# Key differences through all eight steps of an attention unit, and row maxima turned by VectorE and DMAs through DRAM

## The chip, the core and the metric

The kernel runs on one core of a Trainium2 chip. TensorE multiplies matrices, VectorE (DVE), ScalarE (ACT) and GpSimd (POOL) work element by element, and SyncE (SP) issues the DMAs. The metric is the time of the whole program on the device in microseconds, lower is better.

## What is computed

One decoder layer without biases on x of shape (2, 2048, 512) in float32: self-attention with 16 heads of width 32 and rotary angles, a cross-attention of width 77 in the form of two matmuls with a gelu between, and a feed-forward part whose weights are only signs. Each part takes the layer norm of x and is added to x.

```python
x = x + attn(layernorm(x))      # below
x = x + gelu(layernorm(x) @ ctx.T) @ ctx                 # ctx: (2, 77, 512)
x = x + clip((layernorm(x) @ sign(W).T) * scale + bias, -100, 100)

def attn(x):                    # H = 16, DK = 32, S = 2048
    Q = rope(heads(x @ W_q.T)); K = rope(heads(x @ W_k.T)); V = heads(x @ W_v.T)
    scores = Q @ K.T / sqrt(DK)
    return merge(softmax(scores) @ V) @ W_o.T
```

## The kernel before

The work goes batch by batch, and in a batch in two stages: `project_batch` makes Q, K (turned so that the head's 32 values lie on partitions) and V from 16 chunks of 128 tokens; then `Attention.run` goes over 32 *units*. A unit is 256 queries (half of a block of 512) times a group of four heads, which lie on the four quarters of the 128 partitions, so that matmuls of two heads can run beside each other.

A unit has eight *steps* (`STEPS`); step i handles 256 keys: block `i % 4` of 512 keys, chunks 0 and 1 of it in steps 0 to 3, chunks 2 and 3 in steps 4 to 7 (`chunk`). Each step has two halves, heads 0 and 1 first, then heads 2 and 3. A half issues, in this order: the scores of its two heads for the first chunk of keys, the *maxima* matmuls of the other two heads for a later unit, the scores for the second chunk, the exponentials on ScalarE (line 705), the addition of the two chunks' exponentials on GpSimd (`sm`, line 707), the reductions of the maxima on VectorE (line 484), and the matmuls of the step before: `weigh` (weights times values, line 583) and `total` (the softmax's sums, line 597).

The softmax needs the row maxima before the scores. `maxima` therefore computes query times key once more with queries on partitions (line 472), and VectorE reduces each 128x512 tile to one column. This runs `AHEAD` = 10 steps ahead of the scores; the first ten steps of a batch are done by `lead` within and at the end of `project_batch`, whose last stretch is ordered by hand. After the last maximum of a unit `split_maxima` takes the negated maximum of the four blocks (line 491) and splits it on GpSimd into three bfloat16 parts (lines 493 to 497) in `mt`, a tile of 128x2x4x32 whose other entries are zero. `turn_maxima` brings the maxima from columns to rows: one transposing DMA on SP's queue (line 504), and for a batch's first unit two TensorE transposes.

`lower` opens the PSUM tile `st` of a head with a matmul of ones by these rows (line 550), which writes the negated maximum everywhere; `scores` then adds query times key to it. In steps 1 to 3 and 5 to 7 the keys are the differences between a block and the one before (`dk`, made by GpSimd in `key_steps`), so that adding them to what stands in PSUM turns the last step's scores into this step's. Steps 0 and 4 start anew:

```python
if i % NB == 0:
    self.lower(u, heads)
```

PSUM has three tiles for `ps` of the maxima (`ps_s`), four for `st` (`ps_t`), one for `acc`. `divide` takes the reciprocals of the sums on VectorE (line 617). The rest of the layer, `after_attention`, is cut into pieces that `background` slips between the halves: projections (382, 408, 363), norms (327, 137, 138) and the stores. Within `run` the order of TensorE, VectorE, ScalarE and GpSimd is the order of the program text; SP's queue is ordered by the scheduler.

Of the kernel before, what the change touches and what calls it, by code (L numbers as in the profile page):

```python
# [9 lines left out]
F32 = mybir.dt.float32  # L10
F32R = mybir.dt.float32r
BF16 = mybir.dt.bfloat16
AF = mybir.ActivationFunctionType
ALU = mybir.AluOpType
# [11 lines left out]
HQ = 256  # L26
NU = NB * ND * 2
STEPS = NCH // 2
AHEAD = STEPS + 2
SCALE = 1.0 / math.sqrt(DK)  # L30
EPS = 1e-5
MAX_VAL = 100.0
# [4 lines left out]
def decoder_layer(  # L37
# [48 lines left out]

    x_next = [load_x(0, 0), load_x(0, 1)]
    qkv = load_qkv()
    cos = const.tile([P, NCH, DK // 2], F32, tag="cos", name="cos")
    sin = const.tile([P, NCH, DK // 2], F32, tag="sin", name="sin")  # L90
    nc.sync.dma_start(cos, rope_cos.rearrange("(p c) d -> p c d", p=P))
    nc.sync.dma_start(sin, rope_sin.rearrange("(p c) d -> p c d", p=P))

    ident = const.tile([P, P], F32, tag="ident", name="ident")
    make_identity(nc, ident)
# [7 lines left out]
    nc.scalar.activation(minus_half, ones[:, :CPB], AF.Identity, scale=-0.5)  # L103


    mts = []
    for n in range(2):
        mt = const.tile([P, 2, 4, DK], BF16, tag=f"mt{n}", name=f"mt{n}")
        nc.vector.memset(mt, 0.0)
        mts.append(mt)  # L110

    late = {}

# [63 lines left out]

    def project_batch(b, ahead, att, xnt, wk, wq, wv):  # L180
        def times(dst, xnt, w, part=range(ND)):
            for i in part:
                nc.tensor.matmul(dst, xnt[:, i, :], w[:, i, :], start=(i == 0), stop=(i == ND - 1))  # L183

        def transpose_qk(ch, qk, which=(0, 1)):
            blk, c = divmod(ch, CPB)
            cols = slice(c * P, (c + 1) * P)
            for a in which:
                pt = ps_s.tile([P, ND, P], F32, tag="s", name="ptqk")
                for i in range(ND):  # L190
                    nc.tensor.transpose(pt[:, i, :], qk[:, a, i * P : (i + 1) * P], ident)  # L191
                (nc.vector.tensor_copy if a else nc.scalar.copy)((att.q, att.k)[a][blk][:, :, cols], pt)
            if c == CPB - 1 and 1 in which:
                att.open_block(blk)

        def values(ch, xnt, pool=None):
            pv = (pool or ps_s).tile([P, D], F32, tag="t" if pool else "s", name="pv")
            times(pv, xnt, wv)
            keep_values(ch, pv)

        def keep_values(ch, pv):
            v = kvq.tile([P, D], F32, tag=f"v{ch}", name=f"v_{b}_{ch}")
            nc.scalar.copy(v, pv)
            att.v.append(v)


        def rotate(ch, a, ps, r):
            half = [P, H, DK // 2]
            cs = cos[:, ch, None, :, None].to_broadcast(half + [2])
            sn = sin[:, ch, None, :].to_broadcast(half)  # L210
            pairs = ps.rearrange("p (h i t) -> p h i t", i=DK // 2, t=2)
            t1 = r[:, 0, a, :].rearrange("p (h i t) -> p h i t", i=DK // 2, t=2)
            t2 = r[:, 1, a, :].rearrange("p (h i t) -> p h i t", i=DK // 2, t=2)
            nc.vector.tensor_tensor(t1, pairs, cs, ALU.mult)
            nc.vector.scalar_tensor_tensor(
                t2[:, :, :, 0], pairs[:, :, :, 1], -1.0, sn, ALU.mult, ALU.mult
            )
            nc.vector.tensor_tensor(t2[:, :, :, 1], pairs[:, :, :, 0], sn, ALU.mult)  # L218
            nc.gpsimd.tensor_add(r[:, 0, a], r[:, 0, a], r[:, 1, a])  # L219

        held = None
        for ch in range(NCH):
            if ch == (NB - 1) * CPB:
                drain()
            blk, c = divmod(ch, CPB)
            if c == 0:
                att.q.append(kvq.tile([P, ND, BLK], F32, tag=f"q{blk}", name=f"q_{b}_{blk}"))
                att.k.append(kvq.tile([P, ND, BLK], F32, tag=f"k{blk}", name=f"k_{b}_{blk}"))
            r = big.tile([P, 2, 2, D], F32, tag="s", name="r")
            xn = norm(ahead, b, ch + 1) if ch + 1 < NCH else None  # L230
            pk = ps_t.tile([P, D], F32, tag="t", name="pk")
            pq = ps_t.tile([P, D], F32, tag="t", name="pq")
            if ch == NCH - 1:
                break
            times(pk, xnt, wk)
            rotate(ch, 1, pk, r)
            att.lead(1)
            background_between(2)
            times(pq, xnt, wq)
            rotate(ch, 0, pq, r)  # L240
            background_between(2)
            if held is not None:
                transpose_qk(*held)
            held = (ch, r[:, 0])
            xnt_next = turn(xn)
            if ch < NCH - 2:
                values(ch, xnt)
            else:
                left = xnt
            background_between(2)  # L250
            xnt = xnt_next


        ordered = tc.manual_schedule(
            engines={mybir.EngineType.PE, mybir.EngineType.DVE}
        )
        ordered.__enter__()
        times(pk, xnt, wk)
        rotate(ch, 1, pk, r)
        transpose_qk(*held)  # L260
        times(pq, xnt, wq)
        transpose_qk(ch, r[:, 0], (1,))
        rotate(ch, 0, pq, r)
        pv = ps_t.tile([P, D], F32, tag="t", name="pv")
        times(pv, left, wv, (0,))
        att.lead(1)
        times(pv, left, wv, range(1, ND))
        keep_values(ch - 1, pv)
        att.lead(AHEAD)
        values(ch, xnt, ps_t)  # L270
        transpose_qk(ch, r[:, 0], (0,))
        att.split_maxima(0)
        att.turn_maxima(0)
        ordered.__exit__(None, None, None)
        att.key_steps()
# [169 lines left out]
    class Attention:  # L445
# [13 lines left out]
        def maxima(self, n, heads):  # L459
# [25 lines left out]

            return reduce

        def split_maxima(self, u):
            mx = self.mx.pop(u)
            neg = small.tile([P, 2, 4], F32, tag="neg", name="neg")  # L490
            nc.vector.tensor_reduce(neg, mx, AX.X, ALU.max, negate=True)
            mt = mts[u % 2]
            nc.gpsimd.tensor_copy(mt[:, :, :, 0], neg)
            nc.gpsimd.tensor_tensor(neg, neg, mt[:, :, :, 0], ALU.subtract)
            nc.gpsimd.tensor_copy(mt[:, :, :, 1], neg)
            nc.gpsimd.tensor_tensor(neg, neg, mt[:, :, :, 1], ALU.subtract)
            nc.gpsimd.tensor_copy(mt[:, :, :, 2], neg)


        def turn_maxima(self, u):  # L500
            mt = mts[u % 2]
            mrow = small.tile([P, 2, P], BF16, tag="mrow", name="mrow")
            if u > 0:
                nc.sync.dma_start_transpose(mrow, mt.rearrange("p c h d -> p (c h d)"))
            else:
                pt = ps_s.tile([P, 2, P], BF16, tag="s", name="ptm")
                for c in range(2):
                    nc.tensor.transpose(
                        pt[:, c, :], mt[:, c].rearrange("p h d -> p (h d)"), ident_b
                    )  # L510
                nc.vector.tensor_copy(mrow, pt)
            self.mrow[u] = mrow.rearrange("p c q -> p (c q)")

        def key_steps(self):
            self.dk = [None] + [
                const.tile([P, ND, BLK], F32, tag=f"w{n}", name=f"dk{n}") for n in "kqv"
            ]

            def differences(g):
                for kb in range(1, NB):
# [11 lines left out]
            for _ in differences(0):  # L534
                pass
            queue.append(others())


        @staticmethod
# [19 lines left out]
        def scores(self, u, i, heads, c):  # L559
            qb, g, hf = self.units[u]  # L560
            kb, kc = divmod(self.chunk(i, c), CPB)
            keys = self.dk[kb] if kb else self.k[kb]
            for h in heads:
                r = self.rows[h]
                nc.tensor.matmul(  # L565
# [81 lines left out]
        def run(self):  # L647
# [37 lines left out]
            for t in range(NU * STEPS):  # L685
# [10 lines left out]
                pw = big.tile([P, 4, 2, HQ], F32, tag="s", name="pw")  # L696
                sm = sums.tile([P, 4, HQ], F32, tag="sm", name="sm")
                for heads, others in (((0, 1), (2, 3)), ((2, 3), (0, 1))):
                    if i % NB == 0:
                        self.lower(u, heads)  # L700
                    self.scores(u, i, heads, 0)
                    reduce = self.maxima(t + AHEAD, others)
                    self.scores(u, i, heads, 1)
# [6 lines left out]
                    if heads[0] == 0:  # L710
                        first_half()
                        finish()
                        if u >= NU - ND:
                            background(1)
                        elif t % 2 == 1:
                            background(1, light=True)
                    else:
# [3 lines left out]
                            finish()  # L721
                        if (t + AHEAD) % STEPS == STEPS - 1 and u + 1 < NU:
                            self.split_maxima(u + 1)
                            self.turn_maxima(u + 1)
                        background(1)
                prev = (u, i, pw, sm)
            xnt = turn(xn) if more else None
# [9 lines left out]
    xnt = turn(norm(x_next, 0, 0, nc.vector))  # L737
    for b in range(B):
        att = Attention(b)
        project_batch(b, x_next, att, xnt, *qkv)  # L740
        if b == 0:
            late_loads()
        load_ctx(b)
        xnt = att.run()
        if b + 1 < B:
            x_next = att.x_next
            qkv = load_qkv()
    alone.append(True)
    queue += tail
    while queue:  # L750
# [49 lines left out]
```

## Time and profile before

| | before |
|---|---|
| time, median of 3 runs | 2693.01 us (2692.51 to 2693.29) |
| the profiled execution | 2693.15 us, of it 2691.0 us span |
| TensorE clock granted | 0.998 |
| TensorE (PE) busy | 2668.3 us, 99% |
| VectorE (DVE) busy | 1710.0 us, 64% |
| GpSimd (POOL) busy | 1732.8 us, 64% |
| ScalarE (ACT) busy | 1321.0 us, 49% |
| DMA queues of the kernel's data | 4.8% of 16 engines |

The span runs from the first to the last instruction. A matmul's end is modelled, so a busy TensorE is not one at its peak. A line of the timeline gives start and length in microseconds, engine, source line, operation, names of what is written and read, number of instructions merged, and in brackets the idle time before it and what ended it. A line of the groups gives busy time, mean nanoseconds of one instruction, idle time before, and its releasers.

### The profile page before, as it was taken

Reading aid. Unit: us, or ns where it says so; the run is one execution under the profiler, and the core shown is the slowest. Engines: PE = TensorE matmul, PEld = TensorE weight load, DVE = VectorE, ACT = ScalarE, POOL = GpSimd, SP = SyncE. Lnnn points to the kernel's source line nnn. Section 1 sums busy time; section 2 is a strip of 40 time slices with the busy share of each in tenths; the row PEclk is TensorE's granted clock in tenths of the full one; section 3 lists DMA queues with packets and bytes.
Section 4 is the critical chain, followed back from the end, with each engine's and each line's share of the span. In section 5 each row is a group of like instructions: output and inputs, shape, how many; then the busy total and the mean of one; then the engine's idle time right before and its main releaser. Section 6 shows DMA issues by size and latency. Waiting matters only on the chain.

```text
span 2691.0 us, 70222 instructions
## 1 busy us (share of the span) xinstructions
PE 2668.3 (99%) x30756; PEld 1490.3 (55%) x30756; DVE 1710.0 (64%) x2863; ACT 1321.0 (49%) x2394; POOL 1732.8 (64%) x1876
## 2 busy tenths in 40 slices
PE   8999999999999999999999999999999999999998
PEld 4445555555555555555554455555565555555555
DVE  3447777676766766676344477766767667766754
ACT  2115555455546554555422155555555455546553
POOL 3227777567857785677543287766687567857772
PEclk9999999999999999999999999999999999999999
DMA  3010000000000000000201000000000000000000
GB/s 126 24 32 2 5 4 4 4 4 18 20 3 4 12 28 3 4 12 26 73 25 40 5 4 4 4 4 4 4 27 12 4 4 19 19 4 4 19 19 17
DMA packets 38019, 43.54 MB, mean 16 GB/s; under 512 B 20662, under 2 KB 20918, under 8 KB 37712
## 3 DMA queue, kind: packets, MB, share of 16 engines
q1 hardware_dynamic: 37712, 39.05, 4.8%
q8 instruction: 241, 3.95, 0.6%
q14 instruction: 66, 0.54, 0.1%
HBM read 26.58 MB, written 8.39 MB: 13 GB/s over the span
## 4 chain that ended last, share of the span: by engine, by line
PE 98%; DVE 1%; DMA 0%; issue 0%; ACT 0%; POOL 0%; SPq 0%; POOLq 0%; ACTq 0%
PE st L565 23%; PE acc L583 22%; PE ps L472 18%; PE acc L597 8%; PE po L382 4%; PE pk L183 4%; PE pq L183 4%; PE pv L183 4%; PE st L550 3%; PE pf L363 2%; PE pt L345 1%; PE po L408 1%; PE ptqk L191 1%; PE ph L389 1%; PE pt L173 1%; DMA wk<-in_wk_t_dram 0%
## 5 line engine op out<-in xcount | busy, mean ns | idle before, releaser
L707 POOL TENSOR_TENSOR sm<-pw 128x512 f32<-128x512 f32 x1024 | 1295.2, 1272 | 599.5 <-ACT pw L705 596.8
L484 DVE TENSOR_REDUCE mx<-ps 128x1 f32<-128x512 f32 x2048 | 1308.9, 682 | 513.0 <-PE ps L472 509.1
L705 ACT ACTIVATE pw<-st 128x512 f32<-128x512 f32 x2048 | 1111.4, 595 | 947.0 <-PE ps L472 619.4
L472 PE MATMUL ps<-k,q 32*128 32x512 f32 x4096 | 1187.8, 640 | 0.0
L583 PE MATMUL acc<-pw,v 128*32 128x256 f32 x8192 | 655.1, 391 | 0.0
L597 PE MATMUL acc<-sm,ones 128*32 128x128 f32 x7680 | 388.8, 280 | 0.0
L583 PEld LDWEIGHTS acc<-pw,v 128*32 128x32 f32 x8192 | 162.5, 108 | 396.6 <-issue 378.3
L472 PEld LDWEIGHTS ps<-k,q 32*128 32x128 f32 x4096 | 352.4, 183 | 20.2 <-issue 13.8
L597 PEld LDWEIGHTS acc<-sm,ones 128*32 128x32 f32 x7680 | 248.6, 110 | 153.2
L565 PE MATMUL st<-q,dkk 32*128 32x256 f32 x2048 | 291.2, 400 | 0.0
L565 PE MATMUL st<-q,dkq 32*128 32x256 f32 x2048 | 290.0, 400 | 0.0
L565 PE MATMUL st<-q,dkv 32*128 32x256 f32 x2048 | 290.0, 400 | 0.0
L565 PE MATMUL st<-q,k 32*128 32x256 f32 x2048 | 262.8, 375 | 0.0
L565 PEld LDWEIGHTS st<-q,dkk 32*128 32x128 f32 x2048 | 175.8, 184 | 89.5 <-issue 51.3
L565 PEld LDWEIGHTS st<-q,dkq 32*128 32x128 f32 x2048 | 173.0, 184 | 79.9 <-issue 54.1
L565 PEld LDWEIGHTS st<-q,dkv 32*128 32x128 f32 x2048 | 175.0, 184 | 58.6 <-issue 26.3
L565 PEld LDWEIGHTS st<-q,k 32*128 32x128 f32 x2048 | 195.4, 187 | 14.0
L219 POOL TENSOR_TENSOR r<-r 128x512 f32<-128x512 f32 x64 | 81.1, 1268 | 161.8 <-DVE r L218 151.5
L617 DVE RECIPROCAL num<-num 128x128 f32<-128x128 f32 x128 | 120.4, 942 | 53.5 <-ACT num L611 53.5
L137 DVE BATCH_NORM_STATS2 st<-x 128x6 f32<-128x512 f32 x96 | 65.4, 686 | 91.7 <-DMA x<-in_x_dram 91.4
L183 PE MATMUL pk<-wk,xnt 128*128 128x512 f32 x256 | 118.2, 606 | 2.4 <-ACT xnt L175 1.3
L382 PE MATMUL po<-wo,q 128*128 128x512 f32 x256 | 117.4, 603 | 0.0
(109 smaller groups left out, 1784.9 us busy)
## 6 DMA issues: line engine op xcount, KB each, us to landing
x<-in_x_dram SPq DMA_DIRECT2D x64, 256.0 KB, 2.8
out_dram<-x SPq DMA_DIRECT2D x32, 256.0 KB, 2.0
wk<-in_wk_t_dram SPq DMA_DIRECT2D x2, 1024.0 KB, 7.8
wq<-in_wq_t_dram SPq DMA_DIRECT2D x2, 1024.0 KB, 9.9
wv<-in_wv_t_dram SPq DMA_DIRECT2D x2, 1024.0 KB, 5.5
wo<-in_wo_t_dram SPq DMA_DIRECT2D x1, 1024.0 KB, 9.9
wf<-in_wf_t_dram SPq DMA_DIRECT2D x1, 1024.0 KB, 5.0
mrow<-mt SPq DMA_TRANSPOSE x62, 2.3
```

The source lines that it names most:

```text
L183: nc.tensor.matmul(dst, xnt[:, i, :], w[:, i, :], start=(i == 0), stop=(i == ND - 1))
L219: nc.gpsimd.tensor_add(r[:, 0, a], r[:, 0, a], r[:, 1, a])
L382: nc.tensor.matmul(ps, ot[:, i, cols], wo[:, i, :], start=(i == 0), stop=(i == ND - 1))
L472: nc.tensor.matmul(ps, self.q[qb][self.rows[h], g, q0 : q0 + P], self.k[kb][self.rows[h], g, :], start=True, stop=True,)
L484: nc.vector.tensor_reduce(mx[:, qc, h, kb : kb + 1], ps, AX.X, ALU.max)
L550: nc.tensor.matmul(self.st[h], ones_b[r, :], mrow[r, None, :].to_broadcast([DK, 2, HQ]), start=True, stop=False, skip_group_check=True,)
L565: nc.tensor.matmul(self.st[h][:, c, :], keys[r, g, kc * P : (kc + 1) * P], self.q[qb][r, g, hf * HQ : (hf + 1) * HQ], start=False, stop=Tr ...
L583: nc.tensor.matmul(acc[self.rows[h], 0, :], self.v[self.chunk(i, c)][:, d0 : d0 + DK], pw[:, h, c, :], start=(i == 0 and c == 0), stop=(i ...
L597: nc.tensor.matmul(acc[self.rows[h], 1, part], ones, sm[:, h, part], start=False, stop=(i == STEPS - 1), skip_group_check=True,)
L617: nc.vector.reciprocal(num[:, 1, part], num[:, 1, part])
L705: nc.scalar.activation(pw[:, h], self.st[h], AF.Exp, scale=SCALE)
L707: nc.gpsimd.tensor_add(sm[:, hs, :], pw[:, hs, 0, :], pw[:, hs, 1, :])
```

## The change

- `lower` is called in step 0 only. In step 4 the scores use the difference between the first block's second half and the last block's first half (`wrap_around`, made by GpSimd whenever a unit has a new group of heads), so the PSUM tile carries on through all eight steps.
- `AHEAD` is 11 steps. `split_maxima` runs on VectorE instead of GpSimd, in the second half of step 4; `turn_maxima` goes on in the first half of step 5 with a cast and a subtraction on VectorE.
- The split parts lie in a tile of 128x32. VectorE transposes it in squares of 32x32, a DMA writes the result to DRAM (8 KB), and eight DMAs of three rows of 128 values each (in runs of 32) bring it to the rows of `mrow`, which keeps its zeros elsewhere. SP issues all nine. A batch's first unit still uses TensorE.
- The rotary angles no longer have a place of their own: they are loaded anew for each batch into a tile of the pool of `sm`.

```diff
@@ -26,7 +26,7 @@
 HQ = 256
 NU = NB * ND * 2
 STEPS = NCH // 2
-AHEAD = STEPS + 2
+AHEAD = STEPS + 3
 SCALE = 1.0 / math.sqrt(DK)
 EPS = 1e-5
 MAX_VAL = 100.0
@@ -86,10 +86,15 @@
     x_next = [load_x(0, 0), load_x(0, 1)]
     qkv = load_qkv()
-    cos = const.tile([P, NCH, DK // 2], F32, tag="cos", name="cos")
-    sin = const.tile([P, NCH, DK // 2], F32, tag="sin", name="sin")
-    nc.sync.dma_start(cos, rope_cos.rearrange("(p c) d -> p c d", p=P))
-    nc.sync.dma_start(sin, rope_sin.rearrange("(p c) d -> p c d", p=P))
+    def load_angles():
+        angles = sums.tile([P, 2, NCH, DK // 2], F32, tag="sm", name="angles")
+        for n, table in enumerate((rope_cos, rope_sin)):
+            nc.sync.dma_start(angles[:, n], table.rearrange("(p c) d -> p c d", p=P))
+        return angles
+    angles = load_angles()
     ident = const.tile([P, P], F32, tag="ident", name="ident")
     make_identity(nc, ident)
@@ -103,11 +108,18 @@
     nc.scalar.activation(minus_half, ones[:, :CPB], AF.Identity, scale=-0.5)
-    mts = []
-    for n in range(2):
-        mt = const.tile([P, 2, 4, DK], BF16, tag=f"mt{n}", name=f"mt{n}")
-        nc.vector.memset(mt, 0.0)
-        mts.append(mt)
+    def zeros(shape, name):
+        t = const.tile(shape, BF16, tag=name, name=name)
+        nc.vector.memset(t, 0.0)
+        return t
+    first_mt = zeros([P, 2, 4, DK], "first_mt")
+    mts = [zeros([P, 4, DK // 4], f"mt{n}") for n in range(2)]
+    mrows = [zeros([P, 2, P], f"mrow{n}") for n in range(2)]
+    dram = ctx.enter_context(tc.tile_pool(name="dram", bufs=2, space=bass.MemoryType.DRAM))
     late = {}
@@ -177,7 +189,7 @@
-    def project_batch(b, ahead, att, xnt, wk, wq, wv):
+    def project_batch(b, ahead, att, xnt, angles, wk, wq, wv):
         def times(dst, xnt, w, part=range(ND)):
             for i in part:
                 nc.tensor.matmul(dst, xnt[:, i, :], w[:, i, :], start=(i == 0), stop=(i == ND - 1))
@@ -206,8 +218,8 @@
         def rotate(ch, a, ps, r):
             half = [P, H, DK // 2]
-            cs = cos[:, ch, None, :, None].to_broadcast(half + [2])
-            sn = sin[:, ch, None, :].to_broadcast(half)
+            cs = angles[:, 0, ch, None, :, None].to_broadcast(half + [2])
+            sn = angles[:, 1, ch, None, :].to_broadcast(half)
             pairs = ps.rearrange("p (h i t) -> p h i t", i=DK // 2, t=2)
             t1 = r[:, 0, a, :].rearrange("p (h i t) -> p h i t", i=DK // 2, t=2)
             t2 = r[:, 1, a, :].rearrange("p (h i t) -> p h i t", i=DK // 2, t=2)
@@ -485,30 +497,44 @@
             return reduce
         def split_maxima(self, u):
             mx = self.mx.pop(u)
             neg = small.tile([P, 2, 4], F32, tag="neg", name="neg")
             nc.vector.tensor_reduce(neg, mx, AX.X, ALU.max, negate=True)
-            mt = mts[u % 2]
-            nc.gpsimd.tensor_copy(mt[:, :, :, 0], neg)
-            nc.gpsimd.tensor_tensor(neg, neg, mt[:, :, :, 0], ALU.subtract)
-            nc.gpsimd.tensor_copy(mt[:, :, :, 1], neg)
-            nc.gpsimd.tensor_tensor(neg, neg, mt[:, :, :, 1], ALU.subtract)
-            nc.gpsimd.tensor_copy(mt[:, :, :, 2], neg)
+            if u == 0:
+                parts = [first_mt[:, :, :, n] for n in range(3)]
+            else:
+                by_head = mts[u % 2][:, :, 0:6].rearrange("p h (c n) -> p c h n", n=3)
+                parts = [by_head[:, :, :, n] for n in range(3)]
+            nc.vector.tensor_copy(parts[0], neg)
+            nc.vector.tensor_tensor(neg, neg, parts[0], ALU.subtract)
+            self.rest = neg, parts
         def turn_maxima(self, u):
-            mt = mts[u % 2]
-            mrow = small.tile([P, 2, P], BF16, tag="mrow", name="mrow")
-            if u > 0:
-                nc.sync.dma_start_transpose(mrow, mt.rearrange("p c h d -> p (c h d)"))
-            else:
+            neg, parts = self.rest
+            nc.vector.tensor_copy(parts[1], neg)
+            nc.vector.tensor_tensor(parts[2], neg, parts[1], ALU.subtract)
+            mrow = mrows[u % 2]
+            if u == 0:
                 pt = ps_s.tile([P, 2, P], BF16, tag="s", name="ptm")
                 for c in range(2):
                     nc.tensor.transpose(
-                        pt[:, c, :], mt[:, c].rearrange("p h d -> p (h d)"), ident_b
+                        pt[:, c, :], first_mt[:, c].rearrange("p h d -> p (h d)"), ident_b
                     )
                 nc.vector.tensor_copy(mrow, pt)
+            else:
+                square = small.tile([P, DK], BF16, tag="square", name="square")
+                nc.vector.transpose(square, mts[u % 2].rearrange("p h n -> p (h n)"))
+                rows = dram.tile([P, DK], BF16, tag="rows", name="rows")
+                nc.sync.dma_start(rows, square)
+                by_row = rows.rearrange("(a h n) i -> n a h i", a=4, h=4)
+                for h in range(4):
+                    for c in range(2):
+                        nc.sync.dma_start(
+                            mrow[h * DK : h * DK + 3, c].rearrange("n (a i) -> n a i", a=4),
+                            by_row[3 * c : 3 * c + 3, :, h, :],
+                        )
             self.mrow[u] = mrow.rearrange("p c q -> p (c q)")
@@ -517,6 +543,7 @@
             self.dk = [None] + [
                 const.tile([P, ND, BLK], F32, tag=f"w{n}", name=f"dk{n}") for n in "kqv"
             ]
+            self.wrap = None
             def differences(g):
                 for kb in range(1, NB):
@@ -534,6 +561,15 @@
             for _ in differences(0):
                 pass
             queue.append(others())
+        def wrap_around(self, g):
+            if self.wrap is None or self.wrap[0] != g:
+                d = small.tile([P, BLK // 2], F32, tag="wrap", name="wrap")
+                nc.gpsimd.tensor_sub(
+                    d, self.k[0][:, g, BLK // 2 :], self.k[NB - 1][:, g, : BLK // 2]
+                )
+                self.wrap = g, d
         @staticmethod
@@ -559,7 +595,11 @@
         def scores(self, u, i, heads, c):
             qb, g, hf = self.units[u]
             kb, kc = divmod(self.chunk(i, c), CPB)
-            keys = self.dk[kb] if kb else self.k[kb]
+            if i == NB:
+                keys = self.wrap[1][:, None, :].to_broadcast([P, ND, BLK // 2])
+                kc = c
+            else:
+                keys = self.dk[kb] if kb else self.k[kb]
             for h in heads:
                 r = self.rows[h]
                 nc.tensor.matmul(
@@ -696,8 +736,9 @@
                 pw = big.tile([P, 4, 2, HQ], F32, tag="s", name="pw")
                 sm = sums.tile([P, 4, HQ], F32, tag="sm", name="sm")
                 for heads, others in (((0, 1), (2, 3)), ((2, 3), (0, 1))):
-                    if i % NB == 0:
+                    if i == 0:
                         self.lower(u, heads)
+                        self.wrap_around(self.units[u][1])
                     self.scores(u, i, heads, 0)
                     reduce = self.maxima(t + AHEAD, others)
                     self.scores(u, i, heads, 1)
@@ -710,6 +751,8 @@
                     if heads[0] == 0:
                         first_half()
                         finish()
+                        if (t + AHEAD) % STEPS == 0 and u + 1 < NU:
+                            self.turn_maxima(u + 1)
                         if u >= NU - ND:
                             background(1)
                         elif t % 2 == 1:
@@ -721,7 +764,6 @@
                             finish()
                         if (t + AHEAD) % STEPS == STEPS - 1 and u + 1 < NU:
                             self.split_maxima(u + 1)
-                            self.turn_maxima(u + 1)
                         background(1)
                 prev = (u, i, pw, sm)
             xnt = turn(xn) if more else None
@@ -737,7 +779,7 @@
     xnt = turn(norm(x_next, 0, 0, nc.vector))
     for b in range(B):
         att = Attention(b)
-        project_batch(b, x_next, att, xnt, *qkv)
+        project_batch(b, x_next, att, xnt, angles, *qkv)
         if b == 0:
             late_loads()
         load_ctx(b)
@@ -745,6 +787,7 @@
         if b + 1 < B:
             x_next = att.x_next
             qkv = load_qkv()
+            angles = load_angles()
     alone.append(True)
     queue += tail
     while queue:
```

## The prediction

> **What bounds the kernel now.** I read the page first: busy shares, then the chain that ended last.
>
> ```profile
> PE 2668.3 (99%) x30756; PEld 1490.3 (55%) x30756; DVE 1710.0 (64%) x2863; ACT 1321.0 (49%) x2394; POOL 1732.8 (64%) x1876
> PE 98%; DVE 1%; DMA 0%; issue 0%; ACT 0%; POOL 0%; SPq 0%; POOLq 0%; ACTq 0%
> ```
>
> TensorE is the bound, so an edit counts only if it shortens TensorE's stream or makes it wait. Next the timeline of TensorE over a quiet stretch. I call the halves of step i "ia" (heads 0, 1) and "ib" (heads 2, 3); the first line of each half:
>
> ```profile
> 444.27 0.39 PE L550 MATMUL st<-mrow,ones_b 32*128 32x512 bf16 x2
> ...
> 446.24 0.39 PE L550 MATMUL st<-mrow,ones_b 32*128 32x512 bf16 x2
> ...
> 448.21 0.48 PE L565 MATMUL st<-q,dkk 32*128 32x256 f32 x2
> ...
> 450.07 0.49 PE L565 MATMUL st<-q,dkk 32*128 32x256 f32 x2
> ...
> 451.97 0.48 PE L565 MATMUL st<-q,dkq 32*128 32x256 f32 x2
> ```
>
> These are 4a, 4b (with `lower`), 5a, 5b and the start of 6a: 1.97, 1.97, 1.86 and 1.90 us long. Then VectorE and GpSimd from 451 us on:
>
> ```profile
> 451.24 1.29 DVE L484 TENSOR_REDUCE mx<-ps 128x1 f32<-128x512 f32 x2 [0.57 <-PE ps L472]
> 452.63 0.19 DVE L491 TENSOR_REDUCE neg<-mx 128x8 f32<-128x32 f32 x1
> 453.14 1.29 DVE L484 TENSOR_REDUCE mx<-ps 128x1 f32<-128x512 f32 x2 [0.32 <-PE ps L472]
> ```
> ```profile
> 450.75 1.28 POOL L707 TENSOR_TENSOR sm<-pw 128x512 f32<-128x512 f32 x1 [0.79 <-ACT pw L705]
> 452.49 1.27 POOL L707 TENSOR_TENSOR sm<-pw 128x512 f32<-128x512 f32 x1 [0.46 <-ACT pw L705]
> 453.70 0.22 POOL L493 CAST mt<-neg 128x8 bf16<-128x8 f32 x1
> ```
>
> Two things to see. VectorE has a gap of 0.6 us between the reductions of one half and the next (452.53 to 453.14), and that gap lies wholly under GpSimd's addition (452.49 to 453.76). And VectorE has almost no slack: three PSUM banks serve two maxima a half, so the second maximum of a half needs the bank that the first reduction of the half before frees, and in 5b it comes 0.04 us late, which is why 5b takes 1.90 and 5a 1.86. The two reciprocals (L617, 0.94 us each) show the same: they push a half from 1.86 to 2.22. **What VectorE does beyond its 0.6 us gap lengthens TensorE's stream one to one.**
>
> **The change part by part.**
>
> *Lowering once a unit.* 4a goes from 1.97 to 1.86 and 4b from 1.97 to 1.90: 0.11 + 0.07 = 0.18 us, times 64 units = **-11.7 us**. The lowering's share in the chain (L550 3%, 81 us) overstates it, because the maxima of the other two heads run beside it.
>
> *Maxima one step further ahead.* Inside the loop their number only shifts; one step at the end of each batch loses them (1.86 and 1.90 become 1.85, -0.1 us for both). Ahead of the loop one more group of four enters the hand-ordered end of the projection. Batch 1 there:
>
> ```profile
> 1538.86 1.14 PE L472 MATMUL ps<-k,q 32*128 32x512 f32 x8
> 1539.93 3.70 PE L183 MATMUL pv<-wv,xnt 128*128 128x512 f32 x8
> ```
>
> Now two groups follow each other. The second needs the three banks of the first, freed as the reductions (first at 1.16 us, then every 0.6) end: its last matmuls go at about 3.1 us instead of 0, so the values' matmuls start 3.1 us later. In batch 0, 2.4 us by the same reckoning. **+5.5 us**; VectorE's rest is done under the 3.7 us of values.
>
> *The split on VectorE.* Per unit it gets two casts and two subtractions of 128x8 and a 128x32 transpose; GpSimd loses five operations (1.4 us), which TensorE did not wait for. In the changed program's order: negation, cast, subtraction after the reductions of 4b; cast, subtraction, transpose after those of 5a. By their bare durations they fit: the nearest rows are 0.16 us for a subtraction and 0.15 for a one-input operation (below), dependent ones 0.03 apart, and an independent reduction starts 0.08 before its predecessor ends. 4b's gap: 0.19 + 0.16 + 0.16 + 3 x 0.03 - 0.08 = 0.52 of 0.61. For the transpose no row exists: between 0.15 (the smallest operation) and 0.31 (the Trainium skill, VectorE: DVE Perf Modes, The three transpose paths, for four times the width); I take 0.21, and 5a's gap fits too. But the same subtraction looks like this when GpSimd is adding:
>
> ```profile
> 1289.79 1.28 POOL L707 TENSOR_TENSOR sm<-pw 128x512 f32<-128x512 f32 x1
> 1289.85 1.24 DVE L148 TENSOR_TENSOR stats<-stats 128x2 f32<-128x2 f32 x1 [4.21 <-POOL stats L147]
> ...
> 1302.06 1.27 POOL L707 TENSOR_TENSOR sm<-pw 128x512 f32<-128x512 f32 x1 [0.23 <-ACT pw L705]
> 1302.15 1.74 DVE L376 TENSOR_TENSOR x<-x,y 128x512 f32<-128x512 f32 x1
> ```
> ```profile
> 2653.32 0.16 DVE L148 TENSOR_TENSOR stats<-stats 128x1 f32<-128x1 f32 x1 [0.67 <-POOL stats L147]
> 2653.51 0.15 DVE L149 TENSOR_SCALAR stats<-stats 128x1 f32<-128x1 f32 x1
> ```
>
> L148 takes 0.16 us alone and 1.24 under the very addition (L707) that covers our gap; it ends 0.02 after it. L376 takes 0.69 at the end of the kernel and 1.74 here. So a subtraction waits for GpSimd to finish. For the casts the trace has no row; the nearest is L118 (one SBUF input, 128x2048), 1.98 us under a GpSimd addition of which 0.90 were still to run. The Trainium skill (SBUF — State Buffer, Who interferes with whom) says that the pair of ports shared by VectorE and GpSimd is an exclusive lock, taken by two-input VectorE operations and by casts in the two-port mode, and that the later one blocks fully. By the L148 row alone only the subtractions wait; by the rule the casts do too. I work out both.
>
> With casts waiting, times from the start of 5a: reductions of 4b end 0.56, negation 0.78, cast ready 0.82 but GpSimd adds from 0.52 to 1.79: cast 1.81, subtraction 2.00. 5a's first reduction starts at 1.92 instead of 1.17: 5b is **0.75 us longer**. 5a's reductions end at 3.21, GpSimd's next addition runs 2.54 to 3.81: cast 3.83, subtraction 4.02, transpose 4.30 (0.07 for a second wait). 5b's first reduction ends at 4.91, and 6a, which starts at 4.51, waits **0.42 us**. Together 1.17 a unit. Without the casts: 0.57 + 0.40 = 0.97.
>
> In that order 62 units split in the loop. In 37 nothing else stands in either gap: 37 x 1.17 = 43.3. In 13 a batch-norm pair (0.68 + 0.18) follows in 4b, which alone filled its gap: it now starts at 1.92, the reduction at 2.74 instead of 1.23: 13 x 1.5 = 19.5. In 10, 4b holds 2 us of feed-forward matmuls that hide its wait; 5a's remains: 10 x 1.0. Two have no maxima after them. **+72.8 us** (without the casts +63; if 5a's half stayed free, +48).
>
> *The way through DRAM.* What it replaces:
>
> ```profile
> L504 SPq DMA_TRANSPOSE mrow<-mt x62: 1168/1173/1892, 237.4 to 2606.9; - x62
> DMA to landing us min/median/max: 2.3/2.3/4.2
> ```
>
> Now a write and eight reads on SP's queue. A store of 256 KB takes 2.0 us to land and 0.34 to issue, an x load 2.8 and 0.33. Heads 0 and 1 need four reads: 2.0 + 4 x 0.33 + 2.8 = 6.2 us from the transpose; `lower` of 0a comes 8.2 us after it. Heads 2 and 3: 7.5 against 10.2. Zero, with 2 us of cover; a landing as late as the 4.2 above uses it up (both ends: 0, and 0.5 us a unit). Behind the waiting reads on SP stand only out-stores and the x loads after them, which nobody awaits within a few us. The skill speaks against it (the same page's transpose section: a plain DMA that transposes by strides is 19 times slower than the DMA transpose, always use the latter): 19 x 2.3 = 44 us, 36 late, +2200 us in all. I take the rows, since VectorE has turned the squares and each run is 32 neighbouring values.
>
> *The rest.* `wrap`: 40 subtractions of 128x256 on GpSimd, half a 1.27 us addition each, needed four steps later: hidden by GpSimd's 0.5 us a half, and what is left delays a sum used two steps later. The angles for batch 1 queue behind three weights of 1 MB and land about when the first rotation (1332.72) wants them; TensorE then has other matmuls. +0.6 us for both, with lost slack in 4b.
>
> Sum: 2693.15 (the profiled execution; span 2691.0 and 2.15 around it) - 11.7 - 0.1 + 5.5 + 72.8 + 0.6 = 2760.3; that execution is 0.14 over the median, so **2760**.
>
> **The rivals.** *No wait at the ports* (0.10): GpSimd's addition would have to begin after VectorE's gap, at 1.1 us into 5a instead of 0.5, or VectorE be served first. Then only the 13 batch-norm units lose 0.5: 2693 - 11.8 + 5.5 + 6.5 + 0.6 = 2694, no change; with the lead half hidden 2690. Against it are L148 and L376. *Subtractions alone wait* (0.25): 2750. *The rows come late too* (0.08): if a read issued as slowly as the transpose DMA (1.17) and landed after 4.2, heads 0 and 1 would wait 2.0 + 4.7 + 4.2 - 8.2 = 2.7 us, 62 times: 2927. It decides when the nine DMAs take over 8.2 us. *Forecast* (0.57).
>
> **How the numbers follow.** Low end 2733: 5a's half free (48 for 73), with 2 less in the lead. High end 2788: the transpose waiting too (0.3 x 50), late landings now and then (5) and a longer lead (4). Slower by over 0.2% (5.4 us, about what can be told from no change) has the forecast, the second and third rival: 0.90. The first rival is split 0.07 same, 0.03 faster.
>
> **What would show it.** After: `lower` x256 instead of 512; 4a and 4b at 1.86 and 1.90; the casts and subtractions at means near 1 us, ending with L707's successor; 5b near 2.65 and 6a near 2.3; no TensorE wait for `mrow`. Subtractions at 0.16 us would refute it; so would a time under 2710.

## The result, and the profile after

The changed kernel takes **2757.52 us** (median of 4 runs, 2756.92 to 2757.79) against 2692.80 before (4 runs, 2692.51 to 2693.29): 1.024 times as long, 95% interval 1.0222 to 1.0258. The forecast was 2760. The profiled execution's span is 2756.0 us at a granted TensorE clock of 0.998, as before. So the loss is not in the clock.

In the changed kernel the lines are: exponentials 746, addition of `sm` 748, maxima 484, their reductions 496, negation 504, casts 510 and 516, subtractions 511 and 517, square transpose 528, write to DRAM 530, reads 534, `lower` 586, scores 605. The page, TensorE's busy time and the chain that ended last:

```profile
PE 2722.0 (99%) x30500; PEld 1469.0 (53%) x30500; DVE 1842.4 (67%) x3184; ACT 1321.6 (48%) x2394; POOL 1701.9 (62%) x1596
PE 95%; DVE 4%; issue 0%; DMA 0%; ACT 0%; POOL 0%; SPq 0%; POOLq 0%; ACTq 0%
```

TensorE has 256 instructions fewer than before and still ends later; VectorE's share of the chain rose from 1% to 4%, and its busy time by 132 us. What TensorE waits for shows on the weight loads of the maxima, first before, then after (last column: idle time of the weight-load engine, and what ended most of it):

```profile
L472 PEld LDWEIGHTS ps<-k,q 32*128 32x128 f32 x4096 | 352.4, 183 | 20.2 <-issue 13.8
L484 PEld LDWEIGHTS ps<-k,q 32*128 32x128 f32 x4096 | 375.4, 183 | 72.7 <-DVE mx L496 53.4
```

They wait for VectorE's reductions of the maxima, which free the PSUM tiles.

The small operations that are new on VectorE cannot explain its 132 us by their number: 62 units x 5 operations x 0.2 us would be 62 us. The groups by form show what they took (count, then busy us, mean ns); x62 are those in the loop, x2 those of each batch's first unit, which run in the projection, where no addition lies over them:

```profile
L510 DVE CAST mt<-neg 128x8 bf16<-128x8 f32 x62 | 63.3, 1022 | 2.2
L517 DVE TENSOR_TENSOR mt<-neg,mt 128x8 bf16<-128x8 f32 x62 | 28.3, 456 | 2.1
L517 DVE TENSOR_TENSOR first_mt<-neg,first_mt 128x8 bf16<-128x8 f32 x2 | 0.4, 196 | 0.1
L510 DVE CAST first_mt<-neg 128x8 bf16<-128x8 f32 x2 | 0.4, 185 | 0.1
```

The same cast of the same shape takes 0.185 us in one place and 1.02 us in the other. Where, the timeline tells, in a *quiet* unit: one in which TensorE and VectorE have nothing of the background's work in the halves of the split. TensorE, the first matmul of 5a, 5b, 6a and 6b:

```profile
393.79 0.48 PE L605 MATMUL st<-q,dkk 32*128 32x256 f32 x2
...
395.65 0.48 PE L605 MATMUL st<-q,dkk 32*128 32x256 f32 x2
...
398.33 0.48 PE L605 MATMUL st<-q,dkq 32*128 32x256 f32 x2
...
400.58 0.48 PE L605 MATMUL st<-q,dkq 32*128 32x256 f32 x2
```

5a lasts 1.86 us, 5b 2.68 and 6a 2.25 (before: 1.86, 1.90, 1.86; 6a ends in the unit shown for the kernel before with the line below).

```profile
453.82 0.49 PE L565 MATMUL st<-q,dkq 32*128 32x256 f32 x2
```

VectorE and GpSimd over the stretch of the changed kernel:

```profile
394.39 0.19 DVE L504 TENSOR_REDUCE neg<-mx 128x8 f32<-128x32 f32 x1
394.61 1.03 DVE L510 CAST mt<-neg 128x8 bf16<-128x8 f32 x1
395.67 0.17 DVE L511 TENSOR_TENSOR neg<-neg,mt 128x8 f32<-128x8 f32 x1
395.76 1.28 DVE L496 TENSOR_REDUCE mx<-ps 128x1 f32<-128x512 f32 x2
396.96 0.68 DVE L516 CAST mt<-neg 128x8 bf16<-128x8 f32 x1
397.68 0.20 DVE L517 TENSOR_TENSOR mt<-neg,mt 128x8 bf16<-128x8 f32 x1
397.90 0.21 DVE L528 STREAM_TRANSPOSE square<-mt 128x32 bf16<-128x32 bf16 x1
398.04 1.24 DVE L496 TENSOR_REDUCE mx<-ps 128x1 f32<-128x512 f32 x2
```
```profile
394.32 1.28 POOL L748 TENSOR_TENSOR sm<-pw 128x512 f32<-128x512 f32 x1 [0.46 <-ACT pw L746]
...
396.34 1.26 POOL L748 TENSOR_TENSOR sm<-pw 128x512 f32<-128x512 f32 x1 [0.74 <-ACT pw L746]
```

The addition that began at 394.32 ends at 395.60; the cast that was issued under it ends at 395.64. This is so for all 62 first casts of the loop: each begins under an addition and ends 0.04 to 0.05 us after it. The second addition ends at 397.60, the second cast at 397.64. In both places the subtraction behind the cast runs at its bare length, because the addition is over. The reductions of the next half (395.76, 398.04) queue behind the blocked cast, and the matmuls of the maxima behind them.

### The profile page after: what moved, and what is told of

It reads as the page before. It is cut to its first block, busy times and chain, and to the rows that moved or that the text cites. A ratio compares the mean times of both kernels' runs of the same rounds, so it can differ in the third digit from the quotient of the medians.

```text
span 2756.0 us, 70894 instructions
## 1 busy us (share of the span) xinstructions
PE 2722.0 (99%) x30500; PEld 1469.0 (53%) x30500; DVE 1842.4 (67%) x3184; ACT 1321.6 (48%) x2394; POOL 1701.9 (62%) x1596
## 4 chain that ended last, share of the span: by engine, by line
PE 95%; DVE 4%; issue 0%; DMA 0%; ACT 0%; POOL 0%; SPq 0%; POOLq 0%; ACTq 0%
PE st L605 22%; PE acc L623 21%; PE ps L484 19%; PE acc L637 8%; PE po L394 4%; PE pk L195 4%; PE pq L195 4%; PE pv L195 4%; PE pf L375 2%; PE st L586 1%; DVE mx L496 1%; PE pt L357 1%; PE po L420 1%; PE ptqk L203 1%; PE ph L401 1%; DVE mt L510 1%
## 5 line engine op out<-in xcount | busy, mean ns | idle before, releaser
L484 PE MATMUL ps<-k,q 32*128 32x512 f32 x4096 | 1251.9, 639 | 8.3 <-DVE mx L496 8.2
L484 PEld LDWEIGHTS ps<-k,q 32*128 32x128 f32 x4096 | 375.4, 183 | 72.7 <-DVE mx L496 53.4
L605 PE MATMUL st<-q,dkk 32*128 32x256 f32 x2048 | 302.6, 404 | 0.0
L605 PE MATMUL st<-q,wrap 32*128 32x256 f32 x1024 | 144.9, 400 | 0.0
L605 PE MATMUL st<-q,k 32*128 32x256 f32 x1024 | 131.6, 374 | 0.0
```

Source lines behind the costliest of these rows:

```text
L484: nc.tensor.matmul(ps, self.q[qb][self.rows[h], g, q0 : q0 + P], self.k[kb][self.rows[h], g, :], start=True, stop=True,)
L605: nc.tensor.matmul(self.st[h][:, c, :], keys[r, g, kc * P : (kc + 1) * P], self.q[qb][r, g, hf * HQ : (hf + 1) * HQ], start=False, stop=Tr ...
```

## The experiments

Two theories. *Ports* (the name is the prediction's; no trace shows a port): VectorE's casts and two-input operations wait for the GpSimd addition that lies over its gap, and this wait is the loss. *Work:* the split, the transpose and the DMAs through DRAM are simply too much for a gap of 0.6 us, or the lead or the key differences cost the time. Seven kernels tell them apart. The comparison runs of the kernel before gave medians of 2692.86 us for the first four and 2692.56 for the last three.

**The key differences alone.** From the change, with the lead of ten, the split on GpSimd and the transposing DMA put back:

```diff
-AHEAD = STEPS + 3
+AHEAD = STEPS + 2
     # split_maxima and turn_maxima as in the kernel before
```

> The key differences of the change alone (lowering in step 0 only, the copied wrap-around, the angles in the shared buffer); the lead stays ten steps, the split stays on GpSimd and the turning stays one transposing DMA, as before the change. Port theory: the only term of the forecast that is left is the lowering, 64 units x 0.18 us = 11.7 us less than before, 2681 us (2678 to 2685), with 256 lowering matmuls, halves 4a and 4b at 1.86 and 1.90 us, and 5b and 6a at 1.90 and 1.86 us as before. Rival (the loss sits in the key differences themselves: the copied wrap on GpSimd, or the angles that wait for a sums buffer): 2693 us or more, and 5b or 6a longer than before.

Measured: **2682.22 us**, ratio 0.996 (0.9948 to 0.9973), 10.6 us less than before. 4a and 4b take 1.858 and 1.898 us, 5b and 6a are unchanged. This part of the change is a gain, and this kernel is the fastest of all those measured.

**The lead alone.** From the kernel before:

```diff
-AHEAD = STEPS + 2
+AHEAD = STEPS + 3
```

> The kernel before with the maxima led by eleven steps instead of ten, nothing else. The forecast's term for the lead is one more group of maxima in the hand-ordered end of each projection: 2.4 us in batch 0 and 3.1 us in batch 1, so 2698 us (2696 to 2700). Rival (a lead of eleven is free, because that end waits for other things): 2693 us. Rival (the longer lead puts the split of maxima where it delays VectorE in every unit, which is a large part of the 65 us lost): above 2710 us, with 5b or 6a longer than 1.90 us.

Measured: 2700.79 us, ratio 1.003 (1.0018 to 1.0041): 7.9 us more, above the range. The ends of the projections give 2.4 us in batch 0 and 2.6 in batch 1, near the forecast's 2.4 and 3.1. The rest is in the 12 units whose 5b holds a batch-norm unit's matmuls: each is 0.30 us longer. VectorE there, in 4b's gap:

```profile
485.95 0.19 DVE L491 TENSOR_REDUCE neg<-mx 128x8 f32<-128x32 f32 x1
486.05 0.68 DVE L137 BATCH_NORM_STATS2 st<-x 128x6 f32<-128x512 f32 x1
```

With a lead of ten the negation stood in 5b; now it shares a gap with the batch-norm pair, which filled that gap alone. In quiet units the lead costs nothing.

**The split on GpSimd, VectorE's transpose and the way through DRAM kept.** From the change:

```diff
-            nc.vector.tensor_copy(parts[0], neg)
-            nc.vector.tensor_tensor(neg, neg, parts[0], ALU.subtract)
-            self.rest = neg, parts
+            eng = nc.vector if u == 0 else nc.gpsimd
+            eng.tensor_copy(parts[0], neg)
+            eng.tensor_tensor(neg, neg, parts[0], ALU.subtract)
+            eng.tensor_copy(parts[1], neg)
+            eng.tensor_tensor(parts[2], neg, parts[1], ALU.subtract)
     # turn_maxima keeps only the transpose and the DMAs, and moves from 5a to 5b
```

> The change with the two casts and two subtractions of the split on GpSimd (all four in half 4b of the unit), and VectorE's square transpose with the DMAs through DRAM in half 5b. Port theory: VectorE keeps only the reduce and the transpose, neither of which has waited in the changed kernel, so the 72.8 us of port waits go: 2757.5 - 72.8 = 2685 us, up to 2692 if GpSimd's four operations put off its additions; 5b near 1.90 us and 6a near 1.86 us. Rival (VectorE's transpose and the nine DMAs through DRAM are what is dear): 2745 us or more.

Measured: 2693.65 us, ratio 1.0004 (0.9995 to 1.0012), 64 us less than the change. 5b and 6a are 1.897 and 1.858 us again: the negation in one gap and the transpose in another, 0.2 us each, don't lengthen these halves in a quiet unit. It ended 2 us above the expected range. The negation still costs 0.29 us in each of the 12 batch-norm units, 3.5 us in all, as with the lead alone; the expected 2685 had taken this off with the waits. And the rows now came late in some places, from the view of the lowering line (total us, times):

```profile
  DMA mrow<-rows: 3.7, 12
```

Eight units, each behind a unit with feed-forward matmuls, have 0a longer by 0.40 to 0.53 us, 3.6 us together. SP's queue shows why:

```profile
635.34 0.34 SPq L529 DMA_DIRECT2D rows<-square  x1
640.38 0.36 SPq L389 DMA_DIRECT2D out_dram<-x  x1
640.85 2.55 SPq L533 DMA_DIRECT2D mrow<-rows  x8
```

A store of the output stands between the write and its eight reads, and waits for a sum that GpSimd ends at 640.36. In a quiet unit the reads start 1.46 us after the write's issue, here 5.5. So the DMAs themselves are not slow; a queue in which something else waits is. The first two reads are issued by about 641.49 (2.55 / 8 each) and the lowering that needs them runs at 642.74, the next two by 642.13 and theirs waits until 643.28: about 1.2 us from issue to use.

**The additions held back.** The operations of the change on the same engines, but GpSimd's additions of 4b and 5a come after VectorE's pieces, each held by a small copy that reads what VectorE wrote:

```diff
                             self.turn_maxima(u + 1)
+                            seen = small.tile([P, 2, 4], F32, tag="seen", name="seen")
+                            nc.gpsimd.tensor_copy(seen, self.rest[1][2])
+                            nc.gpsimd.tensor_add(sm[:, hs, :], pw[:, hs, 0, :], pw[:, hs, 1, :])
     # likewise after split_maxima, with self.rest[0]
```

> The change as it is, VectorE doing all of the split, but GpSimd's two additions of sums that lay over the split's halves (4b and 5a) come behind it: each is held by a 128x8 copy on GpSimd that reads what VectorE has written last. The same operations on the same engines, two small copies more per unit. Port theory: the casts and subtractions run in 0.16 to 0.29 us each, as those of unit 0 do, 5b falls from 2.68 to about 1.9 us and 6a from 2.25 to about 1.9 us: 2686 to 2696 us. Rival (VectorE's chain of reduce, casts, subtractions, transpose and the eviction work behind it is itself too long for a half, whatever GpSimd does): stays near 2757 us.

Measured: 2703.95 us, ratio 1.0041 (1.0026 to 1.0056): 53.6 of the 64.7 us are gone, though GpSimd has got more to do; 8 us above the expected range. The first cast takes 0.18 us. The second still meets the end of the first addition, which was held and so runs late:

```profile
389.19 0.18 DVE L510 CAST mt<-neg 128x8 bf16<-128x8 f32 x1
390.69 0.41 DVE L516 CAST mt<-neg 128x8 bf16<-128x8 f32 x1
```
```profile
389.79 1.28 POOL L752 TENSOR_TENSOR sm<-pw 128x512 f32<-128x512 f32 x1
```

The second cast ends 0.04 us after the addition. Of the 1.17 us of a quiet unit 0.2 is left, 5.8 us over all of them. The batch-norm units lose 0.79 us each, 9.5 in all (VectorE's work is too long for their gap without any wait, as the last experiment shows), and one unit of each batch still loses 1.4.

**The transposing DMA in place of squares and DRAM.** From the change:

```diff
-                nc.vector.transpose(square, mts[u % 2].rearrange("p h n -> p (h n)"))
-                nc.sync.dma_start(rows, square)
-                # and the eight reads
+                nc.sync.dma_start_transpose(mrow, mt.rearrange("p c h d -> p (c h d)"))
```

> The change with the old way to the rows: VectorE still does the two casts and two subtractions, but one transposing DMA brings the rows, in place of VectorE's square transpose, the write to DRAM and the eight reads. Forecast: the way through DRAM costs nothing and the square transpose only the 0.04 to 0.2 us by which it lengthens the wait at 6a, so 2745 to 2758 us; 5b stays at 2.68 us. Rival (the transpose and the nine DMAs carry a large part of the loss): 2730 us or less.

Measured: 2747.63 us, ratio 1.0204 (1.0189 to 1.022), 9.9 us less than the change. 5b stays at 2.68 us, 6a falls from 2.25 to 2.01 (median; 2.02 in the unit below, whose first matmuls of 5b, 6a and 6b are shown).

```profile
394.42 0.48 PE L588 MATMUL st<-q,dkk 32*128 32x256 f32 x2
...
397.10 0.48 PE L588 MATMUL st<-q,dkq 32*128 32x256 f32 x2
...
399.12 0.48 PE L588 MATMUL st<-q,dkq 32*128 32x256 f32 x2
```

So the transpose costs 0.24 us in most quiet units and in the 14 units with other matmuls in 4b, 9.1 us in all. There it stands behind an operation that waits; with the split on GpSimd, where nothing in front of it waits, it cost nothing. For the nine DMAs nothing is left that can be seen.

**The casts on ScalarE.** From the change:

```diff
-            nc.vector.tensor_copy(parts[0], neg)
+            (nc.vector.tensor_copy if u == 0 else nc.scalar.copy)(parts[0], neg)
     # the same for parts[1]
```

> The change with the two casts of each unit but the first on ScalarE; negation, subtractions and transpose stay on VectorE. Three readings. Casts and subtractions both wait for GpSimd's addition: now the subtraction meets the addition that the cast met, and little is won, by the forecast's sum without waiting casts 0.97 us a quiet unit in place of 1.17, so some 2745 to 2750 us. Only casts wait: the waits are gone, 2690 to 2700 us. The chain from negation to transpose is too long whatever waits in it: two hand-overs to ScalarE and back make it longer still, over 2757 us.

Measured: 2729.64 us, ratio 1.0137 (1.0121 to 1.0154), between the first reading and the second. In quiet units the first reading holds: 5b is 2.46 us and 6a 2.25, 0.95 over before where the forecast's sum had 0.97. Now the subtraction waits for the addition (391.55 to 392.82) that the cast had waited for:

```profile
392.10 0.75 DVE L511 TENSOR_TENSOR neg<-neg,mt 128x8 f32<-128x8 f32 x1 [0.29 <-ACT mt L510]
```
```profile
391.55 1.27 POOL L748 TENSOR_TENSOR sm<-pw 128x512 f32<-128x512 f32 x1 [0.46 <-ACT pw L746]
```

What was not expected is that the 14 units with feed-forward matmuls (8) or cross-attention matmuls (6) in 4b lose nothing, where the forecast had 1.0 us for each of 10. In all 14 the second subtraction and the addition start within 4 ns of each other (below 643.406 and 643.404 us), and the subtraction is not blocked; the addition takes 1.32 us instead of 1.27:

```profile
643.41 0.20 DVE L517 TENSOR_TENSOR mt<-neg,mt 128x8 bf16<-128x8 f32 x1
```
```profile
643.40 1.32 POOL L748 TENSOR_TENSOR sm<-pw 128x512 f32<-128x512 f32 x1 [2.77 <-ACT mt L516]
```

In the changed kernel the subtraction of such a unit comes 0.04 us after the addition's start and takes 1.28 us. Some hundredths of a microsecond decide who waits, and for how long: VectorE over a microsecond, GpSimd 0.05.

**The split by reductions.** From the change, all still on VectorE, in the same places under the same additions:

```diff
-            nc.vector.tensor_copy(parts[0], neg)
-            nc.vector.tensor_tensor(neg, neg, parts[0], ALU.subtract)
+            nc.vector.tensor_reduce(parts[0], mx, AX.X, ALU.max, negate=True)
+            nc.vector.tensor_reduce(pair[:, :, :, 1], parts[0][:, :, :, None], AX.X, ALU.max, negate=True)
+            nc.vector.tensor_reduce(rest[:, :, :, 0], pair, AX.X, ALU.add)
     # parts[1] and parts[2] in the same way
```

> The change with all of the split still on VectorE and at the same places beside GpSimd's additions, but done by reductions alone, which read one operand: a cast is a reduction over one element with a bf16 result, a subtraction a reduction over the pair (value, negated part). That is six small reductions a unit in place of two casts and two subtractions. Port theory (casts and two-input operations wait, a one-input reduction does not): each runs in 0.16 to 0.19 us under GpSimd's additions; the two more than before overfill the gaps of 4b and 5a by 0.1 and 0.2 us, so 2692 to 2712 us. Rival (any VectorE operation on SBUF waits under an addition, or the number of operations is what is dear): 2757 us or more.

Measured: **2699.18 us**, ratio 1.0023 (1.0014 to 1.0032). VectorE has two instructions a unit more than in the change, and the kernel is 58.3 us faster. The second half of the split, and the addition over it:

```profile
390.20 0.18 DVE L531 TENSOR_REDUCE mt<-rest 128x8 bf16<-128x8 f32 x1
390.41 0.17 DVE L532 TENSOR_REDUCE rest<-mt 128x8 f32<-128x8 bf16 x1
390.61 0.19 DVE L536 TENSOR_REDUCE mt<-rest 128x8 bf16<-128x16 f32 x1
390.84 0.21 DVE L547 STREAM_TRANSPOSE square<-mt 128x32 bf16<-128x32 bf16 x1
```
```profile
390.34 1.27 POOL L767 TENSOR_TENSOR sm<-pw 128x512 f32<-128x512 f32 x1 [0.75 <-ACT pw L765]
```

Reductions at 390.41 and 390.61 start and end inside the addition, and so does the transpose. Of the loop's 372 small reductions of the split none took more than 0.20 us. So it is not that VectorE works on SBUF, nor how many operations it has, but which ones. This is what the Trainium skill says (SBUF — State Buffer, Who interferes with whom): casts in the two-port mode contend with GpSimd, and so do operations with two SBUF inputs when GpSimd's reads SBUF, as the addition does; a reduction does not. The mode and the ports are the page's account, the traces show only who waits and until when. Here the price of the difference is 0.17 to 0.19 us against 1.02.

## Why the prediction was right, point by point

- **VectorE's slack (the ground of the sum): right.** What VectorE did beyond its gap came out on TensorE nearly one to one; 5b was to be 2.65 and is 2.68, 6a about 2.28 and is 2.25.
- **Waits at the ports, +72.8: right in cause, and 70.6 us by the lengths of halves 5a to 6b in the two traces.** The terms were off in ways that cancel: 31 quiet units and not 37, at 1.17 on average (36.4 us, not 43.3); 12 batch-norm units at 1.55 (18.6, not 19.5); 14 units with other matmuls in 4b at 0.93 (13.0, not 10.0); two units, one a batch, at 1.4 that the sum did not have. The sum is so near because these cancel, which is luck; the 0.75 and 0.42 us for a quiet unit (0.78 and 0.39 measured) are not. Of the 14, the sum had counted 10, all as feed-forward; 8 are, and 6 hold cross-attention matmuls. That casts wait too was the choice of the rule over the one row of the trace, and the cast of 1.02 us shows it.
- **What of it is waiting:** the version by reductions puts 58.3 us on the waits. VectorE's longer work without waits is the rest: that version stands 9.1 us above 2692.86 - 10.6 + 7.9 = 2690.1, 0.07 us in a quiet unit and, against the run with the split on GpSimd, 0.5 in a batch-norm unit. The latter is the figure that the rival without waits had given for these units. These four measured pieces, -10.6, +7.9, +9.1 and +58.3, sum to +64.7, which is the whole difference; the last two are taken as differences, so this sum is no proof. The lengths of halves 5a to 6b are: from the changed kernel to the one by reductions they fall by 34.3 us in the quiet units, 9.1 in the batch-norm units, 12.2 in the 14 and 2.8 in the two, together 58.4.
- **Lowering, -11.7: -10.6 measured.** 4a fell by 0.11 and 4b by 0.07 as said; but in the 8 units with feed-forward matmuls 4b became 0.07 to 0.11 us longer instead, and 5b of the batch-norm units 0.07 us longer.
- **The rest, +0.5 in sum (last step, wrap-around, angles, slack):** too small to be told from the other terms.
- **Lead, +5.5: 5.0 in the projections' ends.** The negation's move into the batch-norm gap, 3.6 us in the run with the lead alone, was contained in the 1.5 us of these units and not under this heading.
- **The way through DRAM, 0: right.** SP's queue in the unit shown above:

```profile
398.14 0.34 SPq L530 DMA_DIRECT2D rows<-square  x1
399.61 2.51 SPq L534 DMA_DIRECT2D mrow<-rows  x8
```

  The eight reads are issued by 402.12, 4.0 us after the transpose ended, and `lower` comes at 406.20. A read takes 0.31 us to issue, the forecast had 0.33; the write holds the reads up for 1.5 us, not 2.0; and from issue to use it is about 1.2 us by the run with the split on GpSimd, not 2.8. For heads 0 and 1 that is 1.5 + 4 x 0.31 + 1.2 = 3.9 us against the 6.2 of the forecast (its own terms, 2.0 + 4 x 0.33 + 2.8, make 6.1), so the cover is twice as wide as it said. In the loop no TensorE instruction of the changed kernel waits for the rows. The 19 times that the prediction quotes stand in the Trainium skill (VectorE: DVE Perf Modes, The three transpose paths) with a condition that it left out: a plain copy that transposes by strides, when the innermost stride of the destination is large. Here VectorE has turned the squares before and each run is 32 neighbouring values, so no run here tests that figure.
- **The rivals.** *No wait at the ports* gave 2694; the kernels in which the waits are taken away stand at 2693.65 and 2699.18. The first agrees by chance: the split's casts and subtractions are not on VectorE there, and 3.6 us of late rows are in it. *Subtractions alone wait* gave 2750 for a case that did not occur; where only subtractions were left on VectorE, its 0.97 for quiet units held (0.95), but it was too dear by 1.0 us in each of the 14 units with other matmuls in 4b (with the casts on ScalarE the subtractions come at other moments, so that run is near to the case and not the case itself). *Rows late* did not come true here; half a microsecond of it appears in eight units of the run with the split on GpSimd, and not by the slow issue and landing that this rival needed, but by a store that stood in front of the reads.
- **The range:** the three items named for its high end (15, 5 and 4 us over 2760) make 2784, not 2788; the result lies below both.

## What to carry to other kernels

Before small operations are moved into a gap of VectorE, look at what GpSimd does during that gap: a cast of 0.19 us cost 1.02 under a 1.27 us addition, and the queue behind it paid. If they must stand there, write them as reductions (a reduction does both cast and subtraction), or put GpSimd's long operation behind them; best leave them on an engine that nobody waits for. One operand alone is not enough: in the changed kernel a VectorE TENSOR_SCALAR on 128x2 (L161), which reads one, took 1.13 us and ended 0.02 us after the addition that lay over it. And test the parts of a bundle one by one: here one part alone was worth 10.6 us, and the others buried it.

## What the hardware showed beyond the expected

- With the casts on ScalarE, a VectorE subtraction that started within 4 ns of GpSimd's addition took 0.20 us and the addition 0.05 us longer than usual, in all 19 places where this happens, the 14 units with other matmuls in 4b among them. In the changed kernel it started 0.04 us behind the addition in the 14 units and took 1.28 us.
- A blocked cast or subtraction ends 0.03 to 0.06 us after the GpSimd addition, though its own length is 0.17 to 0.20 us.
- The layout of the cast's output made no difference: with neighbouring values 64 bytes apart, as in the kernel with the transposing DMA, the first cast takes 1.02 us on average in the loop, like the 1.02 us of the changed kernel.
- VectorE turned 128x32 bfloat16 in squares in 0.20 to 0.21 us in every kernel that does it, also with an addition under way on GpSimd (in the run by reductions 47 of 62 begin and end inside one, as at 390.84 above): between the two ends that the forecast had for it.
- A VectorE subtraction with one operand in PSUM does not wait: `low`, 128x512, took 0.69 us in the run by reductions (1202.65 to 1203.35), though a GpSimd addition lay over most of it (1201.97 to 1203.24); all 28 of each kernel take 0.62 to 0.69 us.
